# A four-layer graph network on one core: the last tile's 20 nodes in four column groups, and three moves of buffers and sums

## The chip, the cores and the metric

The kernel runs on one core of one Trainium2 chip. The metric is the device time of one execution in microseconds (us). TensorE is called PE, its weight loads PEld, VectorE DVE, ScalarE ACT, GpSimd POOL; SP is the engine that mostly issues loads. [...]

## The reference, cut to what matters

There are 2708 nodes with 512 features each and a dense 0/1 matrix `adj`. Four layers each compute `x = layernorm(x + layer(x, adj))`:

```python
# layer 0
keep = (adj > 0) & (cumsum(adj > 0, axis=1) <= 64)
nb = (keep @ X) / max(keep.sum(1), 1)
y0 = leaky(X @ W_line.T + b_line) + where(cnt > 0, leaky(nb @ W_nb.T + b_nb), 0)
# layer 1
agg = (mask @ x) / max(deg, 1)
y1 = relu(concat(x @ W_self + b_self, agg @ W_nb + b_nb) @ W_comb + b_comb)
# layer 2: attention over adj with 8 heads of 64 (leaky_relu 0.2, softmax)
# layer 3: the same 8 heads, elu; one head of 512, elu; then
out = relu(h @ lin1_w + lin1_b) @ lin2_w + lin2_b          # 512 -> 1024 -> 512
```

## The kernel before

**Tiles.** The nodes are cut into 22 tiles `t` of up to 128 (`P`); the last tile has 2708 - 21 x 128 = 20 nodes. Features stand as 4 (`KD`) blocks of 128, the hidden 1024 of the last linear layers as 8 (`KF`) blocks. A product of a tile with a 512 x 512 weight is four PE products of 512 columns that add up in one PSUM buffer: the tile's transposed features are the stationary operand (128 x number of nodes), a weight block streams. A tile with 20 nodes streams as many columns as a full one. In `product` (line 225) each result goes to the PSUM buffer `pm0` or `pm1`, one each.

**Layer 0, first loop (lines 297 to 324).** Per tile: `X @ W_nb.T` first (linear, so the neighbours are summed after the product), split into two parts `yH` (ACT) and `yL` (DVE, line 223); then `X @ W_line.T` with bias, leaky and the addition of x (lines 315 to 319), stored to `r0_dram` by POOL (line 320). Between them one row block of `adj` is turned into the mask: load by POOL, count on ACT (`count`, line 246), a scan on DVE that drops neighbours after the 64th (`place`, lines 252 and 255, in two halves), transpositions on PE (`turn`, line 264). The second half of `place` is ordered after the last step of the tile's u (`low`). PE's order here is fixed by hand (`pe`).

**Layer 0, aggregation (lines 448 to 476).** For groups of four tiles, PE multiplies the kept mask with yH and yL (line 460). Beside it run the remaining masks, layer 1's weights (`weights1`) and `finish` (line 376) of the group before: it loads r0 through `fetched` into the buffers `rows` of the pool `ahead` (three, shared with all other users of that name), adds bias, leaky, the r0, and normalizes.

**Layer 1.** Lines 481 to 492: per tile two products, with `wnb` (into yH, yL again) and with `wself` (stored as z1). Then the sums over neighbours (line 506).

**Layers 2 and 3, projections (`project`, line 566).** Per tile: the source rows, transposed; eight PE products of 264 columns (line 627); an exp of the attention's target terms (line 605) gathered into the row `vrow` over a whole block of tiles and stored by SP to `v_dram` at the block's end (line 608). From there `v_bc` is broadcast by SP for the attention. Layer 3's source is `summed` (line 929): attention rows `o` are loaded into `rows`, divided, added to x2, normalized in place by ACT, and stored from the same buffer to `x3_dram` by POOL.

**The end.** `last_attention` and `mlp` (line 1007) for pairs of tiles: first linear layer (line 1022) into `gT`, second (line 1031) as eight products per tile into `pl`, then b2 and x3 added, layer norm and the store. The last pair is tile 20 (128 nodes) and tile 21 (20 nodes), in that order.

Except where `pe` or `issue_after` fixes it, a scheduler sets the order of each engine's instructions when the program is built.

Of the kernel before, what the change touches and what calls it, by code (L numbers as in the profile page):

```python
# [18 lines left out]
P = 128  # L19
D = 512  # L20
# [10 lines left out]
def kernel(  # L31
# [57 lines left out]

    o_dram = dram.tile([N, D], F32, name="o_dram")  # L90
    oT_dram, rc_dram = [], []

    behind = []

# [67 lines left out]
    def fetched(src, t, n, pool=ahead, name="rows", bufs=None):  # L162
        x_ = pool.tile([P, D], F32, name=name, bufs=bufs or (3 if pool is ahead else None))
        nc.sync.dma_start(x_[:n], src[t * P:t * P + n, :])
        return x_[:n]
# [19 lines left out]
    def leaky(dst, u):  # L185
        return nc.vector.scalar_tensor_tensor(dst, u, 0.01, u, op0=OP.mult, op1=OP.max)
# [7 lines left out]
    with ExitStack() as phase:  # L194
# [29 lines left out]

        def product(xT, n, w, which, order=as_it_comes):
            pm = ps_mm.tile([P, D], F32, name=f"pm{which}")
            for k in range(KD):
                order(nc.tensor.matmul(pm[:n], xT[:, k, :n], w[:, k, :], start=(k == 0), stop=(k == KD - 1)))  # L228
            return pm
# [45 lines left out]
        with ExitStack() as ph:  # L275
            st = ph.enter_context(tc.tile_pool(name="l0a", bufs=1))
            wnT, wlT = weight(), weight2
            room = [maskT[:, G + k, :4 * D].bitcast(F32) for k in range(2 * KD)]

            xs = rows_of(x)
            xTs = early(0, NT, lambda t, order=as_it_comes: transposed(ahead, ps_tr, xs(t), rows(t), "xT", order))

            transpose_weight(room[:KD], ps_tr, wnT, l0_w_nb)
            lows = {}
            for t in range(2):
                xT = xTs(t, order=pe)
                lows[t] = keep_y(t, P, product(xT, P, wnT, 0, pe))
            transpose_weight(room[KD:], ps_tr, wlT, l0_w_line)  # L290
            b_line = bias(bcast(l0_b_line, D))
            masks = early(1, HERE, lambda i: load_mask(i, st.tile([P, N], BF16, name="m", bufs=3)))
            masks(0)
            nc.gpsimd.memset(maskT[:, NT - 1, :], 0.0)
            nc.gpsimd.memset(maskT[:, :, N:], 0.0)
            counted = turned = 0
            for t in range(NT):
                n = rows(t)
                if t > 1:
                    lows[t] = keep_y(t, n, product(xTs(t, order=pe), n, wnT, 0, pe))  # L300
                xT = xTs(t)
                if t + 1 < NT:
                    xTs(t + 1, order=pe)
                while turned < counted - (t + 1 < NT):
                    for _ in turn(turned, masks(turned), lambda: sums(BF16, (P, G, P)), pe):
                        pass
                    turned += 1
                now = counted < min(HERE, -(-(t - 1) * HERE // (NT - 5)))
                if now:
                    m, places = masks(counted), st.tile([P, N // 2], BF16, name="places", bufs=1)  # L310
                    with tc.issue_after(highs[t].ins):
                        count(counted, m)
# [4 lines left out]
                nc.vector.tensor_add(u[:n], pm[:n], b_line[:n])  # L317
                leaky(u[:n], u[:n])
                low = nc.vector.tensor_add(u[:n], u[:n], xs(t))
# [8 lines left out]
        with ExitStack() as ph:  # L328
# [47 lines left out]
            def finish(ts_, us):  # L376
                for t in ts_:
                    n, u = rows(t), us[t]
                    r0 = fetched(r0_dram, t, n)
                    nc.vector.tensor_add(u[:n], u[:n], b_nb[:n])  # L380
                    leaky(u[:n], u[:n])
                    yield
                    nc.vector.scalar_tensor_tensor(u[:n], u[:n], has[:n, t:t + 1], r0, op0=OP.mult, op1=OP.add)
                    layer_norm(sm, u[:n], n, u[:n])
                    nc.gpsimd.dma_start(x1_dram[t * P:t * P + n, :], u[:n])
                    yield
# [153 lines left out]
        nc.vector.tensor_reduce(pick_c[:, g], rows_c, AX.X, OP.add)  # L540


    LAST, TWIN, few = NT - 1, 32, rows(NT - 1)
    assert few <= TWIN
# [21 lines left out]
    def project(name, source, layer, v_dram, cuts, turned=None, first=None):  # L566
# [12 lines left out]
        with ExitStack() as ph:  # L579
# [7 lines left out]
            width = max(z - a for a, z in cuts) * P  # L587
# [7 lines left out]
            vrows, bs, scaled = {}, {}, {}  # L595

            def keep_v(t):
                n = rows(t)
                a, z = next(c for c in cuts if c[0] <= t < c[1])
                if t == a:  # L600
                    vrows[a] = sm.tile([heads, width], F32, name="vrow", bufs=1)
                vrow = vrows[a]
                ps = ps_v.tile([P, P], F32, name="ps_v")
                nc.tensor.transpose(ps[:heads, :n], bs[t][:n, :heads], ident[:n, :n])
                nc.scalar.activation(vrow[:, (t - a) * P:(t - a) * P + n], ps[:heads, :n], AF.Exp, scale=ALPHA - 1.0)
                if t == z - 1:
                    cols = slice(a * P, a * P + (z - 1 - a) * P + n)
                    nc.sync.dma_start(v_dram[:, cols], vrow[:, :cols.stop - cols.start])

            for t in range(NT):  # L610
                n = rows(t)
# [328 lines left out]
    loads, ready = [], {}  # L940

# [30 lines left out]
    class Last:  # L972
# [34 lines left out]
        def mlp(self, t0, t1, h):  # L1007
            sm = self.sm
            w = sum(rows(t) for t in range(t0, t1))
            if self.pool:  # L1010
                gT = weight().rearrange("p k (f n) -> p (k f) n", n=2 * P)
            else:
                gT = sm.tile([P, KF, 2 * P], F32, name="gT", bufs=1)
            x3s = {}
            for t in range(t0, t1):
                n = rows(t)
                x3s[t] = fetched(x3_dram, t, n, self.pool or sm)
                nc.gpsimd.tensor_add(x3s[t], x3s[t], self.b2[:n])
            for f in range(KF):
                pl = self.ps_l.tile([P, 512], F32, name="pl")  # L1020
                for k in range(KD):
                    nc.tensor.matmul(pl[:, :w], self.lin1[:, k, f * P:(f + 1) * P], h[:, k, :w],  # L1022
                                     start=(k == 0), stop=(k == KD - 1))
                nc.scalar.activation(gT[:, f, :w], pl[:, :w], AF.Relu, bias=self.b1[:, f:f + 1])  # L1024
                if f % 2:
                    yield
            for t in range(t0, t1):
                n = rows(t)
                pl = self.ps_l.tile([P, 512], F32, name="pl")
                for f in range(KF):  # L1030
                    nc.tensor.matmul(pl[:n], gT[:, f, (t - t0) * P:(t - t0) * P + n], self.lin2[:, f, :],  # L1031
                                     start=(f == 0), stop=(f == KF - 1))
                    if f == KF // 2 - 1:
                        yield
                y = (self.pool or sm).tile([P, D], F32, name="xT")
                nc.vector.tensor_add(y[:n], pl[:n], x3s[t])
                layer_norm(sm, y[:n], n, y[:n])
                (nc.sync if t1 == NT else nc.gpsimd).dma_start(out[t * P:t * P + n, :], y[:n])
                yield

    quads = [(t, min(t + 4, NT)) for t in range(0, NT, 4)]
# [385 lines left out]
```

## Time and profile before

| what | value |
|---|---|
| median of three runs | 2994.57 us (2991.03 to 2997.17) |
| profiled execution, its own time | 2990.11 us |
| its span, first to last instruction | 2988.3 us |
| granted TensorE clock, mean | 0.995 |
| PE busy | 2887.4 us (97%), 14456 instructions |
| DVE busy | 1997.9 us (67%) |
| ACT busy | 1533.7 us (51%) |
| POOL busy | 219.8 us (7%) |
| products L228 (layers 0 and 1) | 384 of one weight 177.7 us, 352 of the other 160.2 us |
| last linear layer L1031 | 352 records, 157.4 us |

The chain that ended last is, by share of the span, 64% PE, 21% DVE, 7% ACT, 5% "issue" (nothing to wait for in the profile) and 3% DMA. Busy shares are means over the whole span; the stages differ. Up to about 220 us lies layer 0's first loop, to 500 its aggregation, to 665 layer 1's products, to 884 its neighbour sums, to 977 layer 2's projection, to 1526 its attention, to 1640 layer 3's first projection, to 2185 its attention with 8 heads, to 2268 its second projection, and the rest is the one-head attention with the linear layers.

### The profile page before, as it was taken

What the parts mean: (1) busy time and instruction counts of PE and PEld (TensorE: products, weight loads), DVE (VectorE), ACT (ScalarE), POOL (GpSimd) and SP (SyncE); (2) the same over time, 40 slices, a digit from 0 to 9 for tenths busy, and PEclk for the clock granted to TensorE, in tenths of its full rate; (3) what the DMA queues carried; (4) which work ended last, traced back from release to release, by engine and by line L of the source; (5) the groups of instructions that cost most, each with busy time, mean ns of one, the idle gap of its engine ahead of it and who ended that gap; (6) DMA issues with size and microseconds to landing.
All of it is one profiled execution on the core that took longest, in us unless ns stands there. A gap on an engine that the chain in (4) does not pass through costs nothing.

```text
span 2988.3 us, 36484 instructions
## 1 busy us (share of the span) xinstructions
PE 2887.4 (97%) x14456; PEld 1606.4 (54%) x14456; DVE 1997.9 (67%) x2405; ACT 1533.7 (51%) x1774; POOL 219.8 (7%) x341
## 2 busy tenths in 40 slices
PE   8899999999999999999998999999999999999998
PEld 4447766448888333444466333444475555555555
DVE  6976639413234999999976999999964535445242
ACT  3546533113224999999965899999951000000001
POOL 1110101201110000000022000000000000000000
PEclk9999999999999999999999999999999999999999
DMA  4532325312222011111144111111061000000000
GB/s 120 113 92 59 86 72 143 129 62 85 84 74 80 28 52 39 38 48 44 33 126 140 40 40 39 41 55 46 28 160 60 4 25 14 25 14 15 14 22 20
DMA packets 117426, 180.05 MB, mean 60 GB/s; under 512 B 41042, under 2 KB 65507, under 8 KB 117246
## 3 DMA queue, kind: packets, MB, share of 16 engines
q1 hardware_dynamic: 88974, 116.47, 13.3%
q0 software_dynamic: 18160, 57.39, 6.8%
q10 hardware_dynamic: 10112, 3.77, 0.5%
q8 instruction: 116, 1.90, 0.3%
q14 instruction: 64, 0.52, 0.1%
HBM read 147.55 MB, written 44.65 MB: 64 GB/s over the span
## 4 chain that ended last, share of the span: by engine, by line
PE 64%; DVE 21%; ACT 7%; issue 5%; DMA 3%; POOL 0%; SPq 0%; DVEq 0%; POOLq 0%; ACTq 0%
PE pn L1056 13%; PE po L895 13%; DVE e L703 12%; PE acc L506 7%; PE pm L228 7%; PE pm L627 5%; PE pl L1031 5%; PE pl L1022 5%; ACT c L730 4%; PE acc L460 4%; DVE places L252 2%; PE pd L799 2%; PE ps_tr L124 1%; DMA rows<-o_dram 1%; DVE maskT L485 1%
## 5 line engine op out<-in xcount | busy, mean ns | idle before, releaser
L703 DVE SCALAR_TENSOR_TENSOR e<-v_bc,ucol,maskT 128x1408 f32<-128x1408 f32 (+3 forms) x804 | 1135.6, 1469 | 324.4 <-PE pn L1056 314.3
L730 ACT ACTIVATE c<-e,bcol 128x1300 fp8e4<-128x1300 f32 (+1 forms) x688 | 967.7, 1423 | 75.0 <-DVE e L703 30.0
L895 PE MATMUL po<-e,R 128*64 128x512 f32 (+2 forms) x4224 | 903.8, 547 | 30.2 <-DVE e L703 27.2
L895 PEld LDWEIGHTS po<-e,R 128*64 128x64 f32 x4224 | 338.7, 136 | 562.3 <-issue 396.6
L1056 PE MATMUL pn<-e,R 128*128 128x512 f32 (+1 forms) x1056 | 413.4, 542 | 0.0
L1056 PEld LDWEIGHTS pn<-e,R 128*128 128x128 f32 x1056 | 191.0, 190 | 199.3 <-issue 196.1
L1024 ACT ACTIVATE w<-pl,b 128x256 f32<-128x256 f32 (+1 forms) x88 | 40.9, 465 | 372.9 <-PE pl L1022 364.8
L460 PE MATMUL acc<-yH,kT 128*128 128x512 f32 x484 | 197.3, 408 | 5.0 <-ACT kT L335 5.0
L228 PE MATMUL pm<-w,xT 128*128 128x512 f32 (+1 forms) x384 | 177.7, 606 | 22.1 <-DVE yL L223 18.7
L460 PE MATMUL acc<-yL,kT 128*128 128x512 f32 x484 | 189.3, 391 | 0.0
L506 PE MATMUL acc<-yH,mf 128*128 128x512 f32 x484 | 188.4, 389 | 0.0
L506 PE MATMUL acc<-yL,mf 128*128 128x512 f32 x484 | 188.3, 389 | 0.0
L627 PE MATMUL pm<-w,xT 128*128 128x264 f32 (+1 forms) x704 | 171.1, 398 | 3.6 <-DVE R L656 2.2
L228 PE MATMUL pm<-weight,xT 128*128 128x512 f32 (+1 forms) x352 | 160.2, 598 | 2.3 <-DVE u L317 1.5
L1031 PE MATMUL pl<-lin,w 128*128 128x512 f32 (+1 forms) x352 | 157.4, 592 | 0.0
L1022 PE MATMUL pl<-lin 128*128 128x256 f32 (+1 forms) x704 | 153.4, 371 | 3.7 <-DVE lin L924 3.7
L627 PEld LDWEIGHTS pm<-w,xT 128*128 128x128 f32 (+1 forms) x704 | 131.9, 193 | 30.3 <-ACT xT L126 3.0
L1022 PEld LDWEIGHTS pl<-lin 128*128 128x128 f32 x704 | 129.1, 190 | 34.4 <-issue 15.8
L503 ACT CAST mf<-maskT 128x1024 fp32r<-128x1024 fp8e4 (+1 forms) x66 | 64.4, 977 | 158.0 <-PE acc L506 147.9
L222 ACT CAST yH<-pm 128x512 fp32r<-128x512 f32 (+1 forms) x44 | 25.7, 585 | 229.3 <-PE pm L228 229.3
L335 ACT ACTIVATE kT<-maskT 128x512 fp32r<-128x512 fp8e4 (+1 forms) x132 | 77.5, 594 | 116.6 <-PE acc L460 116.6
L228 PEld LDWEIGHTS pm<-w,xT 128*128 128x128 f32 (+1 forms) x384 | 70.8, 189 | 120.4 <-issue 99.2
(215 smaller groups left out, 2713.1 us busy)
## 6 DMA issues: line engine op xcount, KB each, us to landing
rows<-x_dram SPq DMA_DIRECT2D x63, 256.0 KB
v_bc<-v_dram SPq DMA_DIRECT2D x16, 704.0 KB
x_dram<-u POOLq DMA_DIRECT2D x42, 256.0 KB, 2.4
v_bc<-v_dram SPq DMA_DIRECT2D x16, 650.0 KB
m<-in_adj_dram POOLq DMA_DIRECT2D x13, 677.0 KB, 8.5
rows<-in_x_dram SPq DMA_DIRECT2D x21, 256.0 KB
r_dram<-u POOLq DMA_DIRECT2D x21, 256.0 KB, 3.3
rows<-r_dram SPq DMA_DIRECT2D x21, 256.0 KB
```

The source lines that it names most:

```text
L228: order(nc.tensor.matmul(pm[:n], xT[:, k, :n], w[:, k, :], start=(k == 0), stop=(k == KD - 1)))
L335: made = nc.scalar.activation(kT[:, :w], maskT[:, j, b[0] * P:b[0] * P + w], AF.Relu, scale=-1.0)
L460: nc.tensor.matmul(pa[t], kT[:, (t - b[0]) * P:(t - b[0] + 1) * P], y[:, j, :], start=(j == 0 and y is yH), stop=(j == NT - 1 and y is yL))
L503: nc.scalar.copy(mf[:, :g1 - g0, :], maskT[:, g0:g1, t * P:(t + 1) * P])
L506: nc.tensor.matmul(pa, mf[:, j - g0, :], y[:, j, :], start=(j == 0 and y is yH), stop=(j == NT - 1 and y is yL))
L627: nc.tensor.matmul(pm[a][:m, :D // 2 + heads], xT[:, k, :m], w[:, k, a, :D // 2 + heads], start=(k == 0), stop=(k == KD - 1))
L703: self.made = nc.vector.scalar_tensor_tensor(e[:, :w], v[:, :w], ucol[:, j, h:h + 1], maskT[:, j, c0:c0 + w], op0=OP.max, op1=OP.mult)
L730: nc.scalar.activation(c[:, :w], e[:, :w], AF.Sigmoid, bias=bcol[:, j, h:h + 1], scale=STEP, saturate=False)
L895: pe(nc.tensor.matmul(po[i][HO * k:HO * k + HO, :c1 - c0], R2[:, j, h * HO:(h + 1) * HO], e[:, c0:c1], start=(i_ == 0), stop=(i_ == NT - 1)))
L1022: nc.tensor.matmul(pl[:, :w], self.lin1[:, k, f * P:(f + 1) * P], h[:, k, :w], start=(k == 0), stop=(k == KD - 1))
L1031: nc.tensor.matmul(pl[:n], gT[:, f, (t - t0) * P:(t - t0) * P + n], self.lin2[:, f, :], start=(f == 0), stop=(f == KF - 1))
L1056: nc.tensor.matmul(pn[k][:, :w], R2[:, j, k * P:(k + 1) * P], e[:, :w], start=(j == 0), stop=(j == NT - 1))
```

## The change

1. `product`: for the 20-node tile in layer 1, the four products over `KD` run on four groups of 32 columns of PE at once, each with its own 32 stationary columns (20 nodes and zeros, cleared by POOL) into its own 32 partitions of PSUM. ACT copies the result to SBUF, and one more product with the constant `groups4` sums the four groups.
2. `mlp`: the same for tile 21 in the last linear layer, with eight products in two rounds. The 20-node tile goes first, its sum is taken in the middle of tile 20's products, and its ending follows there.
3. Layer 0: x is no longer added in the first loop; `finish` loads r0 and x and adds them.
4. `keep_v`: each tile's v row is stored by itself, by ACT, from a row of its own (two buffers).
5. `summed`: from tile 2 on, o has three buffers of its own in the projection's pool, and the normalized rows go to `rows`.

```diff
+    few = N - (NT - 1) * P
+    groups4 = const.tile([P, 32], F32, name="groups4")
+    nc.vector.tensor_reduce(groups4, ident.rearrange("p (g n) -> p n g", g=4), AX.X, OP.add)
...
             pm = ps_mm.tile([P, D], F32, name=f"pm{which}")
+            if n == few and order is as_it_comes:
+                nc.gpsimd.memset(xT[:, :, n:32], 0.0)
+                for k in range(KD):
+                    nc.tensor.matmul(pm[32 * k:32 * k + 32], xT[:, k, :32], w[:, k, :], start=True, stop=True)
+                u = sm.tile([P, D], F32, name="u")
+                nc.scalar.copy(u, pm)
+                pm = sums()
+                nc.tensor.matmul(pm[:few], groups4[:, :few], u, start=True, stop=True)
+                return pm
...
-                leaky(u[:n], u[:n])
-                low = nc.vector.tensor_add(u[:n], u[:n], xs(t))
+                low = leaky(u[:n], u[:n])
...
-                    r0 = fetched(r0_dram, t, n)
+                    r0, x0 = fetched(r0_dram, t, n), fetched(x, t, n)
                     nc.vector.tensor_add(u[:n], u[:n], b_nb[:n])
                     leaky(u[:n], u[:n])
+                    nc.vector.tensor_add(r0, r0, x0)
...
-                a, z = next(c for c in cuts if c[0] <= t < c[1])
-                if t == a:
-                    vrows[a] = sm.tile([heads, width], F32, name="vrow", bufs=1)
-                vrow = vrows[a]
+                vrow = sm.tile([heads, P], F32, name="vrow")
...
-                nc.scalar.activation(vrow[:, (t - a) * P:(t - a) * P + n], ps[:heads, :n], AF.Exp, scale=ALPHA - 1.0)
-                if t == z - 1:
-                    cols = slice(a * P, a * P + (z - 1 - a) * P + n)
-                    nc.sync.dma_start(v_dram[:, cols], vrow[:, :cols.stop - cols.start])
+                nc.scalar.activation(vrow[:, :n], ps[:heads, :n], AF.Exp, scale=ALPHA - 1.0)
+                nc.scalar.dma_start(v_dram[:, t * P:t * P + n], vrow[:, :n])
...
-        o, x2 = fetched(o_dram, t, n), fetched(x2_dram, t, n, late, "spare", 2)
+        o = fetched(o_dram, t, n) if t < 2 else fetched(o_dram, t, n, sm, "o", 3)
+        x2 = fetched(x2_dram, t, n, late, "spare", 2)
...
-        layer_norm(late, o, n, o, on_scalar=True)
-        nc.gpsimd.dma_start(x3_dram[t * P:t * P + n, :], o)
-        return o
+        x3 = o if t < 2 else ahead.tile([P, D], F32, name="rows", bufs=3)[:n]
+        layer_norm(late, o, n, x3, on_scalar=True)
+        nc.gpsimd.dma_start(x3_dram[t * P:t * P + n, :], x3)
+        return x3
...
-            for t in range(t0, t1):
+            def end(t, n, pl):
+                y = (self.pool or sm).tile([P, D], F32, name="xT")
+                nc.vector.tensor_add(y[:n], pl[:n], x3s[t])
+                layer_norm(sm, y[:n], n, y[:n])
+                (nc.sync if t1 == NT else nc.gpsimd).dma_start(out[t * P:t * P + n, :], y[:n])
+
+            held = None
+            for t in sorted(range(t0, t1), key=rows):
                 n = rows(t)
                 pl = self.ps_l.tile([P, 512], F32, name="pl")
+                if n == few and self.pool:
+                    nc.gpsimd.memset(gT[:, :, w:w - n + 32], 0.0)
+                    for f in range(KF):
+                        g = 32 * (f % 4)
+                        nc.tensor.matmul(pl[g:g + 32], gT[:, f, (t - t0) * P:(t - t0) * P + 32], self.lin2[:, f, :],
+                                         start=(f < 4), stop=(f >= KF - 4))
+                    held = t, n, self.pool.tile([P, D], F32, name="xT")
+                    nc.scalar.copy(held[2], pl)
+                    continue
                 for f in range(KF):
                     nc.tensor.matmul(pl[:n], gT[:, f, (t - t0) * P:(t - t0) * P + n], self.lin2[:, f, :],
                                      start=(f == 0), stop=(f == KF - 1))
                     if f == KF // 2 - 1:
+                        if held:
+                            got = self.ps_l.tile([P, 512], F32, name="pl")
+                            nc.tensor.matmul(got[:few], groups4[:, :few], held[2], start=True, stop=True)
+                            end(*held[:2], got)
                         yield
...
+                end(t, n, pl)
                 yield
```

More of the change, by code (lines that the diff above doesn't have):

```diff
@@ L91 @@
     oT_dram, rc_dram = [], []
+    few = N - (NT - 1) * P
+    groups4 = const.tile([P, 32], F32, name="groups4")
+    nc.vector.tensor_reduce(groups4, ident.rearrange("p (g n) -> p n g", g=4), AX.X, OP.add)
+    assert few <= 32
     behind = []
@@ L540 @@
         nc.vector.tensor_reduce(pick_c[:, g], rows_c, AX.X, OP.add)
-    LAST, TWIN, few = NT - 1, 32, rows(NT - 1)
-    assert few <= TWIN
+    LAST, TWIN = NT - 1, 32
     nc.sync.dma_start(maskT[TWIN:TWIN + few, LAST, :N], maskT[:few, LAST, :N])
@@ L586, in project @@
                 ps_v, ps_mm = ps_mm, ps_v
-            width = max(z - a for a, z in cuts) * P
             xs = early(1, NT, lambda t: source(sm, t, rows(t)))
@@ L594, in project @@
                 xTs = lambda t: parts(t if t < 3 else (t - 3) // 2 + 3)[:, :, ((t - 3) % 2 if t > 2 else 0) * P:][:, :, :P]
-            vrows, bs, scaled = {}, {}, {}
+            bs, scaled = {}, {}
             def keep_v(t):
                 n = rows(t)
-                a, z = next(c for c in cuts if c[0] <= t < c[1])
-                if t == a:
-                    vrows[a] = sm.tile([heads, width], F32, name="vrow", bufs=1)
-                vrow = vrows[a]
+                vrow = sm.tile([heads, P], F32, name="vrow")
                 ps = ps_v.tile([P, P], F32, name="ps_v")
                 nc.tensor.transpose(ps[:heads, :n], bs[t][:n, :heads], ident[:n, :n])
-                nc.scalar.activation(vrow[:, (t - a) * P:(t - a) * P + n], ps[:heads, :n], AF.Exp, scale=ALPHA - 1.0)
-                if t == z - 1:
-                    cols = slice(a * P, a * P + (z - 1 - a) * P + n)
-                    nc.sync.dma_start(v_dram[:, cols], vrow[:, :cols.stop - cols.start])
+                nc.scalar.activation(vrow[:, :n], ps[:heads, :n], AF.Exp, scale=ALPHA - 1.0)
+                nc.scalar.dma_start(v_dram[:, t * P:t * P + n], vrow[:, :n])
             for t in range(NT):
@@ L1033, in mlp @@
                     if f == KF // 2 - 1:
+                        if held:
+                            got = self.ps_l.tile([P, 512], F32, name="pl")
+                            nc.tensor.matmul(got[:few], groups4[:, :few], held[2], start=True, stop=True)
+                            end(*held[:2], got)
                         yield
[L1035 to L1038, printed above, removed]
+                end(t, n, pl)
                 yield
```

## The prediction

> **What bounds the kernel now.** I read the page, then stretches of 75 us, then the chain of waits inside each stretch that the diff touches. The profiled execution took 2990.1 us (span 2988.3). The table of stretches (columns: stretch, length, busy us and instructions of PE, PEld, DVE, ACT, POOL, then granted clock, DMA share, GB/s):
>
> ```profile
> 75.00:150.00 75.00, 66.98 (x299) 34.19 (x297) 69.70 (x65) 41.49 (x55) 9.51 (x15) 1.00 0.55 113
> 600.00:675.00 75.00, 75.00 (x220) 36.73 (x219) 12.43 (x18) 10.71 (x19) 5.63 (x11) 1.00 0.20 61
> 1575.00:1650.00 75.00, 63.34 (x279) 44.79 (x279) 52.83 (x158) 43.36 (x96) 18.59 (x35) 0.93 0.39 128
> ```
>
> Layer 0's first loop (0 to 220 us) leans on DVE, layer 1's products (500 to 665) on PE, and in layer 3's projection (1526 to 1640) nobody is full: something else is waited for. The chain through one turn of layer 0's loop (start us, length, what):
>
> ```profile
> 112.53 0.69 DVE u L317
> 113.25 0.70 DVE u L186
> 113.97 0.69 DVE u L319
> 114.67 2.95 DVE places L252
> 117.61 0.58 DVE yL L223
> 118.19 0.79 DVE m L255
> 119.03 0.05 issue
> 119.07 2.99 DVE places L252
> 122.12 0.75 issue
> 122.87 0.69 DVE u L317
> ```
>
> DVE is never idle in this turn of 10.34 us (the "issue" of 0.75 is its L255 product), so each instruction taken out shortens the turn. Now layer 3's projection: its chain, and who held SP's queue from 1510 to 1650 us (total, times, longest):
>
> ```profile
> 1553.90 3.67 DMA rows<-o_dram
> ...
> 1563.47 3.95 DMA rows<-o_dram
> ...
> 1573.45 3.87 DMA rows<-o_dram
> ```
>
> ```profile
> SPq L164 <- DMA x_dram<-rows: 34.4, 12, 6.7
> ```
>
> The o rows are normalized in their own buffer and stored from it; only when that store has landed may SP load o into it again. Three buffers do not cover store plus load. Last, the end:
>
> ```profile
> 2938.67 13.73 PE pl L1031 x32
> 2952.41 8.05 PE pl L1022 x64
> 2960.46 13.86 PE pl L1031 x32
> 2974.32 0.02 issue
> 2974.34 0.69 DVE xT L1036
> ```
>
> Two records are one fp32 product of 512 columns (0.86 us). The last 13.86 us are tile 20 and then tile 21, which costs the same for 20 nodes; DVE's ending follows.
>
> **The change part by part** (negative is time gained).
>
> *x added in layer 0's finish instead of its first loop.* L319 (690 ns) leaves DVE in 14 turns that the chain runs through: 14 x 0.70 = -9.7. The rebuilt order also puts the second L255 product (0.79) ahead of yL; where PE then waits for yL (the chain goes yL to pm at 90.97, 149.35 and 197.42) that costs 3 x 0.79 = +2.3. Is something next? The turn becomes 9.6; PE's own work in it, 108.00 to 117.07 in the timeline, is 9.1, and a mask load lands 8.5 us after issue, so both fit, narrowly. POOL's r0 store and the mask load behind it on its queue move up with the leaky step. **-7.4**; bounds -9.7 (yL costs nothing) and -2 (masks or PE hold the old pace).
> What it adds: 22 sums r0 + x (0.69 each, 15 us) and 22 loads of 256 KB on SP. 18 lie under layer 0's PE-bound aggregation, where DVE has long waits (47.4 us at one L485, 43.1 for L246). The last four fall between 500 and 560 us, where DVE is full to 550 (10.00 of each 10) and PE already loses 1.1 + 0.2 + 1.5 us. Summing DVE's order between one yL and the next, the heaviest before is 10.4, afterwards 8.4, 7.8 and 7.7, against PE's turn of 7.3: about even. But r0, x and the x1 rows share three buffers, so an x1 load must wait for the transposition of the row before it: one turn (7.3) ahead instead of two; loads take 3 to 4. I take **+1**, between -2 and +6.
>
> *Layer 1's products of the last tile.* Before: 8 products x 0.86 = 6.9 on PE. After, twice: one round of four groups (0.86), a wait for ACT's copy (0.58 and two handovers, 0.9), one sum over the groups (0.86), in all 5.2. The second clearing by POOL waits for the first round and stands behind two z1 stores (0.73 each), about 2.0 after the round before it, hidden under 2.6. ACT issues two weight loads (8 took 5.42 us, 0.68 each) between, which may hold yH back 0.5, not PE. **-1.5** (-1.7 to 0).
>
> *v stored per tile.* 66 stores on ACT instead of 9 on SP. Each waits for its exp, then costs queue time: the nearest row is rc_dram's store on ACT, 0.33. ACT has 1.5 of 4.1 us per tile busy in layer 2's projection; xT comes 3 us early. Only from tile 16 on, where ACT is full with e's sigmoids, do 6 stores count, partly under ecol and ucol: +0.7 in layer 2, the same inside the next figure for layer 3, and about +0.3 at the end of layer 3's second projection, where the last R waits on ACT. In return a 3.3 us wait of ACT for a v store goes. The Trainium skill speaks against this: DMA: Bandwidth & Descriptors, section "Measured (HBM→SBUF, 128 partitions, SWDGE, issued from GpSimd)", tells to batch, transfers under 64 KB being dominated by descriptors, and its section on one DMA's anatomy gives about 2.0 us fixed (for GpSimd's path). 57 more stores by that price would be 114 us if each were waited for; by the row they are 57 x 0.33 = 19 us of ACT, nearly all beside PE, and two vrow buffers give each store a whole tile (3.6 to 4.1 us) to land. The row decides: **+1.0** (0 to +3).
>
> *Own buffers for o, x3 apart.* From tile 2 on, an o load waits for ACT's normalization of three tiles before, not for a store. Loop: load 4, sums and normalization 4.5, over three buffers, 2.9 a tile. PE then sets the pace. Its price is in layer 2, whose same products run at 930.90 - 926.79 = 4.11 a tile. Tiles 3 to 15 start here from 1542.65 to 1599.63, 57.0 for 12; at 4.11, 49.3: -7.7. DVE (3.2 busy plus 0.7 waiting for POOL's power) fits just under. After tile 15, up to the first po at 1640.46, three PE waits follow these loads (2.4, 2.1, 0.5), and products beside them run at a granted clock of 0.8 to 0.9 (5.41 instead of 3.73; 10.38 instead of 7.5); but ACT (30.6 of 40 us) and DVE are near full, and v_bc now stands behind tile 19's o on SP. I take -3.5 of 9.6. Only two o rows are fetched early instead of three; the third lands about 1532, its products start near 1538, as before. **-11** (-4 to -17).
>
> *Last linear layer.* Tile 21's 8 products in two rounds, 1.7 for 6.9; plus 0.86 for the sum. ACT's copy hides under tile 20's first half (3.4), tile 21's ending under its second. But POOL's clearing of gT waits for ACT's last relu, and the first round for it: PE stops 0.85 where it now runs on. Tile 20's ending closes the kernel as long as tile 21's did (3.1), its store of 256 KB lands like the others (2.3). -6.9 + 1.7 + 0.86 + 0.85 = **-3.4** (-4.3 to -1.5). Do fp32 groups run side by side? The nearest rows, PE's timeline:
>
> ```profile
> 1519.37 2.40 PE L895 MATMUL po<-e,R 128*64 128x512 f32 x12
> 1657.14 1.47 PE L799 MATMUL pd<-c,parts_c 128*12 128x384 fp8e4 x32
> ```
>
> Two heads of 1408 fp32 columns take 2.40, what one alone would (2.75 x 0.86). The 32 narrow products take 1.47; L506 passes 512 columns in 0.227 (219.64 us for 968), so 384 in 0.17, and eight rounds of four are 1.36, one after the other over 5. So two fp32 groups share the time, and so do four narrow ones. Against it the Trainium skill, TensorE: Matmul & The Clock Gate, "Measured speedup vs the span model": three column groups gave 2.38, not 3. By that rate a round is 1.26 times as long: 2.2 instead of 1.7 here, 0.2 twice in layer 1, 0.9 us less gained. The rows (1.01 and 1.08) disagree; I keep them.
>
> Three small clearings (0.13 each by L620's like) and one sum of the identity at the start lie on idle engines. Sum: -7.4 + 1 - 1.5 + 1.0 - 11 - 3.4 = **-21.3**. The profiled execution is 4.5 below the median of the three runs (2994.6); I take the difference from the median: **2973.3**.
>
> **Rivals.**
> 1. Layer 3's projection stays bound elsewhere: DVE in order (3.9 of 4.11 a tile) or loads at 190 GB/s and more. For: DVE waits in 18 places for POOL's power. Against: layer 2's pace, DVE 6.5 of 10. Then -4 instead of -11: 2980.3.
> 2. Four fp32 groups share nothing (four different streams). For: no fp32 row with four. Against: pd's four, po's two. Layer 1 becomes 2 x (3.4 + 0.9 + 0.9) = 10.4, +3.5; the end 6.9 + 0.9 + 0.85 - 6.9 = +1.7: sum -11.2, 2983.4.
> 3. Slower: the three row buffers starve PE between 220 and 560 us. SP is in order, and each tile of finish now takes two buffers; the eight weight rows for layer 1 and the x1 rows of tiles 1 to 10 are behind them, and PE's order is fixed. A starved row costs a load and its transposition, 4 us or so. Other gains are 22; from 6 starved rows the change is worth nothing, all 18 would give +50. For: SP already stands 23 us over the four W_nb rows. Against: PE waited only 0.3 us for such a row. With ten: +18, 3013.
> 4. Layer 0's turn stays at its pace (mask loads): -2 instead of -7.4, 2978.7.
>
> **How the numbers follow.** The forecast as summed 0.60, rival 1 0.15, rival 4 0.11, rival 2 0.07, rival 3 0.07. The forecast's own bounds, added by chance rather than all one way, are about 12 either side (2962 to 2985); the range 2959 to 2987 takes in rivals 1, 2 and 4. A difference of 0.2% (6.0 us) is about what this measurement can tell from none. Faster by more: nearly all of the forecast and rivals 1, 2 and 4, 0.87; within: 0.08; slower: 0.05.
>
> **What would show it.** Right: layer 0's turn near 9.6 with no L319; L627 in layer 3's projection every 4.1 us and SP's wait for x_dram stores gone; the end with one 1.7 us round of four groups, then tile 20's 6.9 around one sum. Wrong: PE waiting for rows in 220 to 560 us; L627 still every 4.6 or more; a round of four groups near 3.4.

## The result, and the profile after

The changed kernel takes **2976.07 us** (median of five runs, 2972.27 to 2979.11) against 2995.59 us before (median of five, 2991.03 to 2998.87): a ratio of 0.9938 with a 95% interval of 0.9926 to 0.9949, or 18.6 us less (15.3 to 22.2). The prediction said 2973.3, 21.3 less. So the sign, the size and the range were right. Of its six terms three were near, those of x's loop, of layer 1 and of the end. The term for x in `finish` missed its mechanism, and the terms for v and o were right in their sum but not in how it is divided between them.

One caution ahead of the traces. The profiled execution of the changed kernel took 2979.11 us, the slowest of its five, and that of the kernel before 2990.11, less than any of its five. The two spans (2977.2 and 2988.3) therefore differ by only 11.1 us. About 5 us of the missing gain were lost in the first 40 us. There PE's first eight records of weight products took 6.62 us in the profile after and 3.70 in the one before, and another group of eight 5.40 instead of 3.70. In the second group the clock granted between 28 and 32 us is 0.59. In the first the records follow each other every 0.85 us, as the slow ones of the second group do, though the profile's clock column says 1.00 there; why they are slow is not shown. Nine of the twelve profiles of this study show 3.70 for the first of these groups, eight of them of kernels with part or all of the change, so I take this for a matter of the execution and not of the change. I compare stages, from one landmark (PE's first instruction of a stage) to the next, rather than spans.

The same three stretches as in the prediction (columns: stretch, length, busy us and instructions of PE, PEld, DVE, ACT, POOL, then granted clock, DMA share, GB/s), after:

```profile
75.00:150.00 75.00, 70.68 (x315) 36.55 (x316) 68.56 (x60) 41.78 (x56) 9.46 (x15) 1.00 0.59 123
600.00:675.00 75.00, 73.52 (x229) 36.98 (x228) 13.86 (x21) 12.75 (x22) 5.85 (x13) 1.00 0.20 61
1575.00:1650.00 75.00, 66.97 (x348) 45.69 (x348) 56.28 (x155) 52.28 (x101) 15.88 (x33) 1.00 0.34 111
```

In layer 0's loop PE is busier (70.68 us instead of 66.98) and over these 75 us now a little fuller than DVE (68.56). In the turn shown next DVE still sets the pace: it is busy for 9.46 of the 9.56 us, PE for 8.73. In 600 to 675 PE now has the short waits of the four-group products. In layer 3's projection PE rises from 63.34 to 66.97 us, and the granted clock from 0.93 to 1.00.

One turn of layer 0's loop after the change (DVE's timeline: start us, length, engine, line, operation, tiles):

```profile
120.30 0.68 DVE L230 TENSOR_TENSOR yL<-pm,yH 128x512 fp32r<-128x512 f32 x1
120.90 2.97 DVE L268 TENSOR_TENSOR_SCAN places<-m,over 128x1354 bf16<-128x1354 bf16 x1
123.90 0.86 DVE L271 TENSOR_TENSOR m<-m,places 128x1354 bf16<-128x1354 bf16 x1
124.68 0.68 DVE L333 TENSOR_TENSOR u<-pm,bias 128x512 f32<-128x512 f32 x1
125.40 0.69 DVE L193 SCALAR_TENSOR_TENSOR u<-u 128x512 f32<-128x512 f32 x1
126.01 3.03 DVE L268 TENSOR_TENSOR_SCAN places<-m,places,over 128x1354 bf16<-128x1354 bf16 x1
129.08 0.86 DVE L271 TENSOR_TENSOR m<-m,places 128x1354 bf16<-128x1354 bf16 x1
129.86 0.68 DVE L230 TENSOR_TENSOR yL<-pm,yH 128x512 fp32r<-128x512 f32 x1
```

From yL to yL it is 9.56 us; before, 10.34. The sum with x is gone and yL stands behind the second L271 product, as the prediction had it. SP's waits for row loads (L171) between 1510 and 1650 us no longer name a store of x3. The longest are now for ACT's normalization, which frees o's own buffers, and for a step of the layer norm on DVE:

```profile
SPq L171 <- ACT rows L125: 20.7, 10, 3.3
...
SPq L171 <- DVE ln_rs L119: 11.0, 11, 2.0
```

And the end, PE's timeline (two records are one fp32 product of 512 columns):

```profile
2944.62 8.22 PE L1034 MATMUL pl<-lin 128*128 128x148 f32 x64
2952.77 1.92 PE L1053 MATMUL pl<-lin,w 128*32 128x512 f32 x16
2954.62 3.70 PE L1059 MATMUL pl<-lin,w 128*128 128x512 f32 x8
2958.25 1.04 PE L1064 MATMUL pl<-xT,groups 128*20 128x512 f32 x2
2959.22 3.70 PE L1059 MATMUL pl<-lin,w 128*128 128x512 f32 x8
```

Eight products of 20 nodes take 1.85 us (2952.77 to 2954.62) in two rounds of four groups, where the kernel before needed 6.9, and PE does not stop between the first linear layer and them.

The landmarks of both profiles (po and pn are the products of the attentions with 8 heads and with one, den the sums that divide pn):

| stage, from its first product to the next landmark | before, us | after, us | difference |
|---|---|---|---|
| start to first aggregation product | 220.72 | 218.72 | -2.0 (of it about +5 by the slow products at the start) |
| layer 0's aggregation, to layer 1's first product | 280.93 | 283.39 | +2.5 |
| layer 1's products, to the first neighbour sum | 163.06 | 161.66 | -1.4 |
| neighbour sums | 220.87 | 220.87 | 0 |
| layer 2's projection, to the first po product | 91.39 | 95.99 | +4.6 |
| layer 2's attention | 551.10 | 550.55 | -0.5 |
| layer 3's projection, to its first po product | 112.39 | 99.85 | -12.5 |
| layer 3's attention and second projection | 627.64 | 629.45 | +1.8 |
| one-head attention, to the last den product | 670.16 | 670.16 | 0 |
| the end, to PE's last product | 36.04 | 32.28 | -3.8 |

Two rows go the wrong way by more than the prediction's terms for them (+1 and +0.7): layer 0's aggregation and layer 2's projection. The experiments start from these.

### The profile page after: what moved, and what is told of

Same layout as the page of the kernel before. It is cut to its first block, busy times and chain, and to the rows that moved or that the text cites. A ratio compares the mean times of both kernels' runs of the same rounds, so it can differ in the third digit from the quotient of the medians.

```text
span 2977.2 us, 36614 instructions
## 1 busy us (share of the span) xinstructions
PE 2878.1 (97%) x14462; PEld 1604.0 (54%) x14462; DVE 1995.6 (67%) x2406; ACT 1535.9 (52%) x1775; POOL 217.9 (7%) x344
## 3 DMA queue, kind: packets, MB, share of 16 engines
q1 hardware_dynamic: 91952, 121.83, 13.8%
## 5 line engine op out<-in xcount | busy, mean ns | idle before, releaser
L120 POOL TENSOR_TENSOR ln_rs<-ln_rs,half 128x1 f32<-128x1 f32 (+1 forms) x88 | 57.9, 658 | 1464.6 <-DVE ln_rs L119 1396.0
L1059 PE MATMUL pl<-lin,w 128*128 128x512 f32 x336 | 150.8, 593 | 0.0
L636 PEld LDWEIGHTS pm<-w,xT 128*128 128x128 f32 (+1 forms) x704 | 127.9, 187 | 29.3 <-ACT xT L133 3.4
```

The source lines that it names most:

```text
L636: nc.tensor.matmul(pm[a][:m, :D // 2 + heads], xT[:, k, :m], w[:, k, a, :D // 2 + heads], start=(k == 0), stop=(k == KD - 1))
```

## The experiments

Each kernel's times are compared with runs of the kernel before on the same chip; gains in us are (1 - ratio) times the median before (2994.0 to 2994.5). The letters A, B and C stand for the theories in the expectations.

**The parts, each put alone into the kernel before.** First the sum with x:

```diff
-                leaky(u[:n], u[:n])
-                low = nc.vector.tensor_add(u[:n], u[:n], xs(t))
+                low = leaky(u[:n], u[:n])
...
-                    r0 = fetched(r0_dram, t, n)
+                    r0, x0 = fetched(r0_dram, t, n), fetched(x, t, n)
...
+                    nc.vector.tensor_add(r0, r0, x0)
```

> The kernel before with one part of the change alone: x is added in layer 0's finish (r0 + x) instead of its first loop. Theory A (from the profile after): the turn of the first loop falls from 10.34 to about 9.56 us, some 7.8 us in all, but the first r0 + x sum stands on DVE ahead of tile 21's bias sum and waits there some 7 us for x's load; kT's copies on ACT stand behind it, PE stops about 3.7 us instead of 2.1 near 220 us and part of its next products runs at a low clock. Net gain 4 to 6 us: about 2990.5. Theory B (the prediction as written): the loop gives 7.4, finish takes 1, no such stop: gain 6.4, about 2989. Theory C: the first loop gains only the 2.0 us by which its end came earlier in the profile after: about 2993.5. A and B are told apart by the trace: DVE's wait for in_x_dram's rows before the first r0 + x sum, and PE's stop there.

Measured: 2989.41 us, ratio 0.9984 (0.9977 to 0.9991), 4.8 us less (2.7 to 6.9). The time does not tell A from B; the trace does. The first aggregation product starts at 213.76 instead of 220.72, in an execution whose first rows came 0.46 later: 7.4 us gained in the loop, so C is out. Then DVE's timeline shows what A says:

```profile
209.68 0.68 DVE L223 TENSOR_TENSOR yL<-pm,yH 20x512 fp32r<-20x512 f32 x1 [2.80 <-ACT yH L222]
217.25 0.69 DVE L381 TENSOR_TENSOR rows<-rows 128x512 f32<-128x512 f32 x1 [6.89 <-DMA rows<-in_x_dram]
217.86 0.67 DVE L317 TENSOR_TENSOR u<-pm,bias 20x512 f32<-20x512 f32 x1
```

and PE's:

```profile
215.50 0.40 PE L460 MATMUL acc<-yL,kT 128*128 128x512 f32 x1
219.47 0.50 PE L460 MATMUL acc<-yH,kT 128*128 128x512 f32 x1 [3.58 <-ACT kT L334]
```

L381 is the first r0 + x. The brackets give the idle time before an instruction and who ended it. DVE waits 6.89 us for the load of x; tile 21's own bias sum (L317), which before the change ran 4.2 us after the same yL, now stands behind it. That sum frees the bias buffer into which ACT is to load `b_nb`, and behind that load on ACT stand the kT copies for which PE waits. A second stop of PE, of 1.58 us, follows; before, there was a single one of 2.10.

Why did x come late? Its load stands on SP behind that of the r0 row:

```profile
209.55 0.35 SPq L164 DMA_DIRECT2D rows<-r_dram  x1
209.99 0.38 SPq L164 DMA_DIRECT2D rows<-in_x_dram  x1
```

SP's waits put the time before the first of these down to a store of r0 (`DMA r_dram<-u`, 33.6 us), which POOL had issued at 207.17 for tile 20. PE had read the last row out of `rows` at 201.79, so the three buffers were not what x waited for. x itself needs no store; it is only second in SP's order. It then took 7.2 us to land, beside two loads of `adj` rows (677 KB each, at a DMA share of 0.92).

The stage as a whole hardly shows this: 281.09 us from the first aggregation product to layer 1's first, against 280.93 before. But the profile before has a low clock near 402 us (0.50 for 3.41 us) that this one does not have. The kernel with the column groups alone (below), whose aggregation is that of the kernel before, has no low clock there either and takes 279.36. Measured by that, the cost is about 1.7 us. Another 2.6 us are lost in layer 3's projection (115.03 us instead of 112.39), which this edit does not touch; the kernel with the columns alone shows the same (114.83). Of these some 2 us are a longer stop ahead of po (3.49 and 3.48 instead of 1.36), and why it is longer there is open.

**v stored per tile**, alone:

```diff
-                if t == a:
-                    vrows[a] = sm.tile([heads, width], F32, name="vrow", bufs=1)
-                vrow = vrows[a]
+                vrow = sm.tile([heads, P], F32, name="vrow")
...
-                if t == z - 1:
-                    nc.sync.dma_start(v_dram[:, cols], vrow[:, :cols.stop - cols.start])
+                nc.scalar.dma_start(v_dram[:, t * P:t * P + n], vrow[:, :n])
```

> The kernel before with one part alone: v stored per tile, on ACT's queue, from two vrow buffers. Theory A: the exp of tile 21 in layer 2's projection needs the buffer that tile 19's store is still reading, so it is put behind a sigmoid, two table loads and ecol on ACT; layer 2's first po product starts 4 to 5 us later than before, and layer 3's second projection loses about 1 more: 5 to 6 us slower, about 3001. Theory B (the prediction): ACT's queue time alone, 1.0 us slower, about 2996.6. Theory C: nothing (2995.6), the later start of po being taken up by DVE's pace in the attention.

Measured: 2992.0 us, ratio 0.9997 (0.9989 to 1.0006): no difference that the times can tell, between 3.3 less and 1.8 more. A's stop is there, 4.78 us of PE ahead of layer 2's first po product, and 95.99 us for the stage instead of 91.39. But A's total is refuted, and so is C's reason: layer 2's attention does not take the stop up (550.26 us instead of 551.10). What gives it back is layer 3's projection: 107.24 us instead of 112.39. Of these 5.1 us about 3.4 are time at a low clock (6.8 us lost to it before, 3.4 here, summed over windows of 4 us as length times one minus the granted clock). The two kernels that leave this stage as it was, x in `finish` and the columns alone, take 115.03 and 114.83 us with 3.4 and 5.1 lost to the clock. So 107.24 is less than the scatter of these three gives, and the clock is not all of it. What in the stage became shorter was not traced.

**v and o together:**

```diff
-        o, x2 = fetched(o_dram, t, n), fetched(x2_dram, t, n, late, "spare", 2)
+        o = fetched(o_dram, t, n) if t < 2 else fetched(o_dram, t, n, sm, "o", 3)
+        x2 = fetched(x2_dram, t, n, late, "spare", 2)
...
+        x3 = o if t < 2 else ahead.tile([P, D], F32, name="rows", bufs=3)[:n]
```

> The kernel before with v stored per tile and with own buffers for o and x3 in layer 3's projection (own o buffers alone do not fit in SBUF beside the wide vrow). Theory A: layer 3's projection becomes 12.5 us shorter, as in the profile after, and the v stores cost 5 to 6 elsewhere: gain about 6 to 7, 2989. Theory B (the prediction): 11 gained, 1 lost: gain 10, about 2985.6. In the trace L616's like runs every 4.1 us in layer 3's projection under both; layer 2's first po product tells A from B.

Measured: 2987.2 us, ratio 0.9967 (0.9954 to 0.9979), 9.9 us less (6.3 to 13.8). B's number is the nearer one, but both lie in the interval. Layer 3's projection takes 100.84 us, 11.5 less than before, and layer 2's stays at 95.99: A's two halves, with less lost elsewhere than A thought.

**The four column groups**, both places, in the kernel before (the two blocks of the diff in `product` and `mlp`).

> The kernel before with the four column groups alone, in layer 1's products and in the last linear layer. Theory A (prediction and profile after): one round of four takes about 0.95 us in place of four products at 0.86; layer 1 gains 1.4 to 1.5, the end 3.4 to 3.8: gain 5, about 2990.5. Theory B (the groups share nothing, the profile after being a matter of modelled ends): 5 us slower, about 3000.8.

Measured: 2988.13 us, ratio 0.9980 (0.9971 to 0.9989), 6.0 us less (3.3 to 8.7). A holds, B is out: layer 1's products take 161.32 us instead of 163.06, and the end 32.28 instead of 36.04, together 5.5.

The three kernels gain 4.8 + 9.9 + 6.0 = 20.7 us; the whole change gained 18.6 by its ratio. The parts add up within their intervals.

**The late po of layer 2.** ACT's timeline of the changed kernel shows what stands ahead of it:

```profile
974.98 0.27 ACT L616 ACTIVATE vrow<-ps_v 8x128 f32<-8x128 f32 x1
...
975.28 0.27 ACTq L617 DMA_DIRECT2D v_dram<-vrow  x1
...
975.78 0.27 ACT L616 ACTIVATE vrow<-ps_v 8x128 f32<-8x128 f32 x1
...
976.16 1.28 ACT L739 ACT_TABLE_LOAD   x1
977.46 1.47 ACT L739 ACTIVATE c<-e,bcol 128x1408 fp8e4<-128x1408 f32 x1
978.95 1.28 ACT L649 ACT_TABLE_LOAD   x1
...
980.42 0.16 ACT L616 ACTIVATE vrow<-ps_v 8x20 f32<-8x20 f32 x1
```

and PE's next instruction:

```profile
980.63 2.42 PE L904 MATMUL po<-e,R 128*64 128x512 f32 x5 [4.78 <-ACT vrow L616]
```

Before, the last two exps stood side by side:

```profile
976.58 0.33 ACT L605 ACTIVATE vrow<-ps_v 8x128 f32<-8x128 f32 x2
```

Here tile 21's (8x20, at 980.42) comes 3.8 us later, behind a sigmoid and two table loads. My reading was that it needs the vrow buffer that tile 19's store, issued at 975.28, is still reading, so that the scheduler, which orders ACT when the program is built, puts other work first. The test is one more buffer and nothing else:

```diff
-                vrow = sm.tile([heads, P], F32, name="vrow")
+                vrow = sm.tile([heads, P], F32, name="vrow", bufs=3)
```

> The changed kernel with three vrow buffers instead of two, nothing else. Theory A (the late po of layer 2 comes from the buffer: the exp of tile 21 waits for tile 19's store, and so stands behind a sigmoid, two table loads and ecol on ACT): the exp moves ahead of the sigmoid, layer 2's first po product starts about 92 us after the first product of its projection instead of 96.0, and with the low clock behind that stop gone the kernel is 4 to 6 us faster than the changed one: about 2971 (ratio to before 0.992). Theory B (it comes from ACT's time for the stores themselves): po still starts some 96 us after, 2976. Theory C: po starts earlier, but the attention gives it back, being paced by DVE: 2975 to 2976.

Measured: 2971.69 us, ratio 0.9928 (0.9915 to 0.9941), and the stage takes 91.63 us. PE's timeline:

```profile
970.56 0.38 PE L615 MATMUL ps_v<-ident,b 128*8 128x128 f32 x2
971.36 1.94 PE L904 MATMUL po<-e,R 128*64 128x512 f32 x8 [0.41 <-ACT vrow L616]
```

The 66 stores on ACT are all still there, so B is out; the attention does not give the gain back (550.19 us), so C is out. It was the buffer, not the queue time of the stores. The medians are 4.4 us apart, which alone the intervals would not prove; the landmark is what shows it.

**The early r0 + x.** In the changed kernel, the sum is ordered behind the leaky step of its own tile:

```diff
-                    leaky(u[:n], u[:n])
-                    nc.vector.tensor_add(r0, r0, x0)
+                    low = leaky(u[:n], u[:n])
+                    with tc.issue_after(low.ins):
+                        nc.vector.tensor_add(r0, r0, x0)
```

> The changed kernel with the sum r0 + x ordered behind the leaky step of the same tile on DVE, nothing else. Theory A: DVE no longer waits 6.9 us for x's load ahead of tile 21's bias sum, kT's copies come in time, PE's stop of 3.7 near 220 us becomes the 2.1 of before: 1.5 to 2 us faster, and up to 2.5 more where the stop was long enough to lower the clock: 2972 to 2975. Theory B: the stop stays, since kT's copies wait for something else (b_nb's load issued by ACT, whose buffer tile 21's bias sum frees): 2976.

Measured: 2971.79 us, ratio 0.9929 (0.9916 to 0.9942). DVE's wait for x is gone, and with it the stop of 3.67 us; but a stop stays:

```profile
222.59 0.79 PE L477 MATMUL acc<-yH,kT 128*128 128x512 f32 x1 [2.96 <-ACT kT L350]
```

ACT counts a mask there (2.55 us), and waits 1.28 for that mask's load first. In the changed kernel PE stops 1.43 us for the same mask, part of it being hidden behind the first stop: 3.67 + 1.43 became 2.96. Layer 0's aggregation goes from 283.39 to 280.61 us, 2.8 less and within A's bounds. B is out, since ACT's load of b_nb no longer waits.

**Both mended:**

> The changed kernel with both: three vrow buffers, and r0 + x behind the leaky step. If the two stops are separate (Theory A of both), the gains add up: 6 to 9 us faster than the changed kernel, 2967 to 2970, ratio to before 0.990 to 0.992. If either is given back later: 2971 to 2976.

Measured: **2967.55 us** (2966.73 to 2972.31), ratio 0.9916 (0.9903 to 0.9929). This is 8.5 us under the changed kernel by the medians and 6.6 by the ratios, whose intervals just touch. The landmarks agree: layer 0's aggregation takes 279.65 us (283.39 in the changed kernel), layer 2's projection 91.63 (95.99). A little is given back: layer 1's products take 162.95 us instead of 161.66.

**And v by GpSimd in the second projection of layer 3:**

> As the last, and in layer 3's second projection (one head) v is stored through GpSimd's queue instead of ACT's. Theory A: ACT, which also scales R there, is what held that projection 0.8 to 0.95 us longer than before the change (84.24 us against 83.29 from its first product to the first pn product); without the stores it is back at 83.3: 0.9 faster than the last, below what the times can tell but plain in the trace. Theory B: a random stop of that profile; no difference.

Measured: 2973.14 us, ratio 0.9931 (0.9920 to 0.9943). A is refuted: from that projection's first product to the small product `pk` behind it, it takes 85.90 us, with the stores on ACT 85.61, and PE still waits there for ACT's R. Before the change it took 83.05, with v per tile alone 82.86. So taking these stores off ACT does not mend the 1 to 3 us. That does not clear them altogether: with all v stores issued by SP (below) the same stretch takes 82.62. The cause stays open. This kernel's median is 5.6 us over the last one's, though the intervals overlap. Of the 8.2 us between the two profiled executions (2974.92 and 2966.76) about 5 are low clock: it is at 0.50 for 13.7 us of this one and for 3.4 us of the other.

**Which queue, and how many buffers.** The changed kernel with its v stores issued by SP:

```diff
-                nc.scalar.dma_start(v_dram[:, t * P:t * P + n], vrow[:, :n])
+                nc.sync.dma_start(v_dram[:, t * P:t * P + n], vrow[:, :n])
```

> The changed kernel with the 66 v stores issued by SP instead of ACT, nothing else. It asks whether it is the queue that matters. Theory A: SP works in order and carries the o and x2 loads of layer 3's projection; a store there waits for its exp and holds the loads behind it, so that projection (first product to first po) goes from 99.9 to 103 or more, while layer 2's late po stays (two vrow buffers, some 96 us): 2979 or more. Theory B: with o's own buffers the loads run far enough ahead, and ACT is relieved of 66 issues: 99 to 101 us there, 2974 to 2976.

Measured: 2979.26 us, ratio 0.9957 (0.9940 to 0.9973): A by the trace, where layer 3's projection takes 106.23 us instead of 99.85 (the intervals of the two ratios overlap). SP stands for its stores (between 1510 and 1650 us):

```profile
SPq L617 <- ACT vcol L671: 21.1, 4, 8.9
...
SPq L617 <- ACT ucol L658: 11.2, 6, 4.6
```

But loads held back are only part of it. Half of the 6.4 us is one longer stop ahead of po, 4.73 us where the changed kernel has 1.51:

```profile
1632.71 7.49 PE L904 MATMUL po<-e,R 128*64 128x512 f32 x26 [4.73 <-ACT vrow L616]
```

Tile 21's exp stands there once more behind a sigmoid and two table loads on ACT, as in layer 2.

And the changed kernel with two own buffers for o instead of three (`"o", 3` becomes `"o", 2`):

> The changed kernel with two own buffers for o instead of three, nothing else. Theory A (the prediction's loop: a load of 4 us plus 4.5 of sums and normalization, over the number of buffers): 8.5 / 2 = 4.25 a tile against PE's 4.11, so layer 3's projection gets longer by some 18 x 0.14 = 2.5 us, from 99.9 to about 102.5; 2978.5. Theory B: the loads take longer than 4 where three rows are asked for at once, and two buffers starve PE as before the change: 108 or more, 2984. Theory C: no difference, PE's pace is met either way: 2976.

Measured: 2985.17 us, ratio 0.9971 (0.9961 to 0.9981): B. The stage is back at 112.10 us. SP's o loads come in pairs (its other loads are left out here):

```profile
1551.76 2.98 SPq L171 DMA_DIRECT2D o<-o_dram  x2
1560.39 3.23 SPq L171 DMA_DIRECT2D o<-o_dram  x2
1569.32 3.23 SPq L171 DMA_DIRECT2D o<-o_dram  x2
1578.47 3.51 SPq L171 DMA_DIRECT2D o<-o_dram  x2
1588.70 2.97 SPq L171 DMA_DIRECT2D o<-o_dram  x2
1598.60 0.32 SPq L171 DMA_DIRECT2D o<-o_dram  x1
```

Ten rows in 46.84 us (1551.76 to 1598.60) are 4.68 a tile, where the prediction's way of reckoning (8.5 us over the number of buffers) gives 4.25 for two and PE needs 4.11. On top of that the clock is low again beside waits of 1 to 2 us near the end of the stage: 3.4 us are lost to it there, 1.6 at the stage's start. The whole gain of this part hangs on the third buffer: to store x3 from a buffer apart is not enough with two for o. Three for o without the separate x3 was not tried.

## Why the prediction was right, point by point

- **x out of the first loop, -7.4: right.** The turn is 9.56 us (9.6 predicted), the loop gives 7.4 in the single-part kernel. Rival 4 (the turn keeps its pace) is out.
- **x in finish, +1: a mechanism was missed.** The prediction counted the sums and loads between 220 and 560 us and looked for the loss at 500. The loss is at 220, where the very first r0 + x, free to go early, was put ahead of tile 21's bias sum on DVE. It is about 1.7 us in the kernel with this part alone and 2.5 by the table in the changed one, where a low clock followed the stop. That +1 is near this is luck. The part gained 4.8 us where -7.4 + 1 promised 6.4, which its interval still holds. Rival 3 (rows starve PE) looked in the right direction, SP's order and late rows, but one late row did the harm and not ten, and it was late for a store and not for a full ring: between 300 and 525 us PE is as busy as before (221.6 us instead of 220.7 over three stretches).
- **Layer 1 in four groups, -1.5: right,** -1.4 in the changed kernel and -1.7 with the columns alone. Rival 2 is out.
- **v per tile, +1.0: the sum was right and its working wrong.** For layer 2 the mis-sized term is the one by which "6 stores count", +0.7: it is +4.6. The prediction gave each store "a whole tile (3.6 to 4.1 us) to land" with two buffers. That fails at tiles 19 to 21, whose exps crowd together when the last products are done. Against it stands layer 3's first projection, 5.1 us shorter with v alone, where the prediction put another +0.7 into o's figure. The part alone is worth 0.9 us less, within 3.3 less and 1.8 more. The +0.3 in the second projection was not seen with v alone.
- **The price of small transfers.** By the Trainium skill (DMA: Bandwidth & Descriptors, "Anatomy of one DMA — SWDGE (gpsimd) path"), about 2.0 us are fixed for each, on GpSimd's path; the estimate of 114 us came from that. With v alone the kernel is the same within 3.3 us, so the row of 0.33 us was the right base (before there are 10 stores, not 9, so 56 more and not 57; nothing rests on it); what a small store cost was a buffer held until it had landed, in one place.
- **Own buffers for o, -11: the mechanism was right, the size partly luck.** The stage went from 112.39 to 99.85 us, 12.5 less, and tiles 5 to 15 run at 42.18 / 10 = 4.22 us (1554.53 to 1596.71), near the 4.11. Rival 1 (DVE or the loads stay the bound) is out. But two errors cancel: tiles 3 to 15 give 5.1 us (51.84 instead of 57.0) where I took 7.7, and from tile 15 to the first po it is 34.3 instead of 40.8, so 6.5 where I took 3.5. Nor is all of it o's: v alone already takes 5.1 off this stage, so o's share of it is 6.4 (107.24 to 100.84). By the ratios v and o give 9.9 and v alone 0.9, so o about 9, by the medians (2992.0 and 2987.2) 4.8; both intervals are several us wide. The loop over the buffers was too kind: for two buffers it gives 4.25 and 4.68 was measured. (8.5 over three is 2.8, not 2.9; nothing rests on that.)
- **The end, -3.4: right, -3.8.** The 0.85 us stop for POOL's clearing does not exist: POOL clears the columns at 2944.91, with no wait for ACT's relus, 7.9 us ahead of the first group product. Two rounds take 1.85 instead of the 1.7 assumed, and the sum 0.97 instead of 0.86. A round of four is thus 0.93 us against 0.86 for one product, 1.08 times as long, as pd's row said. The estimate of 1.26 times, from the three groups in the Trainium skill (TensorE: Matmul & The Clock Gate, "Measured speedup vs the span model"), was too dear.

## What to carry to other kernels

Count a ring of buffers for the moment when its users come closest together, not at their mean pace: two vrow buffers were enough for twenty tiles and cost 4.6 us at the last, and a third buffer for o was worth 9 us (2985.17 against 2976.07). Work that is taken off a full engine and put "somewhere later" needs a place in the order: a sum that waits for a load may be put ahead of work that is ready, and then everything behind it on that engine waits too. The same holds for the load: x stood behind a row that waited for a store. When two profiles differ by less than the times, compare stage by stage between landmarks, and part by part in kernels of their own. Then look at what the stages that nobody touched did: layer 3's projection moved by 2.6 us in two kernels that left it alone.

## What the runs showed of the hardware

A stop of PE can cost more than itself. With the 4.7 to 4.8 us stop at layer 2's po, all six profiles that have it show a granted clock of 0.50 to 0.70 in a window of 4 us at its end or close behind; the six without the stop (0.3 to 0.4 us) show none there. In the aggregation near 220 us, where PE is the bound, it costs time. The windows of the changed kernel (same columns as the first table):

```profile
220.00:224.00 4.00, 0.82 (x4) 0.36 (x2) 1.71 (x3) 0.00 (x0) 0.00 (x0) 0.91 1.07 222
224.00:228.00 4.00, 3.51 (x8) 2.81 (x9) 0.25 (x1) 1.14 (x3) 0.56 (x1) 0.50 0.30 91
228.00:232.00 4.00, 3.96 (x13) 2.78 (x11) 0.68 (x1) 2.35 (x3) 0.00 (x0) 0.73 0.32 80
```

Products follow each other there every 0.43 us instead of 0.23. It isn't certain: the same stop of 3.58 us in the kernel with x in finish brought no low clock at all, one of 2.96 did, and so did one of 2.43.

The low clock has a fixed length. Once PE's work has begun and up to its end, all twelve traces show it at 0.50 for 3.41 us or for 6.83, twice that. With the window set to one of them, in the kernel before:

```profile
1606.92:1610.33 3.41, 3.41 (x9) 2.64 (x8) 2.05 (x7) 1.25 (x4) 0.88 (x2) 0.50 0.22 87
```

By half of each, it takes at most 1.7 or 3.4 us of PE's time. The Trainium skill (TensorE: Matmul & The Clock Gate, "Part 1: The HAM clock gate") tells of a free-running window of about 3.4 us whose idleness halves the clock. The halved clock, the 3.41 us and the chance in it agree with that; the stops of 2.43 and 2.96 us that were enough are shorter than the window. In layer 3's projection the kernel before lost 6.8 us to the low clock, and the changed kernel none. One of the windows of the kernel before:

```profile
1628.00:1632.00 4.00, 4.00 (x12) 3.21 (x13) 1.46 (x3) 3.94 (x10) 1.10 (x3) 0.50 0.06 16
```

So part of the 12.5 us is not the waits themselves but the low clock that came with them. It is probably also a reason why two executions of one kernel differ by several us: of 37 executions of the kernel before, the fastest (2987.78 us) had a mean granted clock of 0.997, the slowest (2999.53) 0.994.
